# Moving the small loads, copies and GpSimd work of a two-layer attention kernel to the heads of their blocks

## The chip, the cores and the metric

The kernel runs on one core of a Trainium2 chip. The metric is the device time of one execution, in microseconds (us); times of several executions are given by their median. The engines are named as the profile names them: PE (TensorE, matmuls; PEld is its weight load), DVE (VectorE), ACT (ScalarE), POOL (GpSimd), and SP, which here only issues DMAs.

## The reference

The input x is 1 x 32 x 128 x 256 in float32: 4096 tokens of 256 numbers. Layer 0 is an attention over all tokens that is masked by the time index t (0 to 127), with 8 heads of 32; layer 1 is a windowed attention followed by 8 small networks ("experts") with a soft choice between them. Cut to what matters:

```python
# layer 0: h is x, 4096 tokens
q   = layernorm(h) @ wq.T + bq + sym_emb[n]
Q   = q @ wQ.T + bQ ;  K = h @ wK.T + bK ;  V = h @ wV.T + bV      # 8 heads
s   = Q K^T / sqrt(32), -inf where t(key) > t(query)
h   = h + alpha * (softmax(s) V @ out_w.T + out_b)
# layer 1: t is h as 32 sequences of 128 tokens
xl  = layernorm(t)
z   = (relu(xl K xl^T + bias) - 10000 outside a band of 24) * temperature
t   = t + softmax(z) xl
xf  = layernorm(t);  w = softmax(mean over sequences(xf) @ Wr + br)  # 8 experts
for e in range(8):
    a = relu(batchnorm(xf @ W1[e] + b1[e])); a = relu(batchnorm(a @ W2[e] + b2[e]))
    t = t + w[e] * (a @ Wo[e] + bo[e])
```

## The kernel before

**Layer 0.** The tokens are reordered by time, so that the mask is nearly block triangular, and the 4096 queries are taken in 8 blocks b of 512 columns (BLK). The heads are two groups g of four. A unit (b, g) goes over the key tiles of 128 keys that its block may see; one key tile of one group is a step. Both units of block 0 make 6 steps, those of the later blocks 13, 21, 29, 37, 45, 53 and 61.

The order of all engines' work is written out by hand: one loop with the counter n issues, at each round,

- `scores(n)`: 16 matmuls (L1330), those of the first head into the PSUM tile sa (one bank, one buffer), those of the other three into sb (three banks, two buffers);
- `product(n-2)`: 8 or 16 matmuls of the exponentials with the values (L1420), into av;
- `exps(n)`: ACT's two exponentials of sa (L1343) and sb (L1345) into pt, a ring of five SBUF buffers; in a step on the diagonal, POOL then sets the masked parts of pt to zero (L1357);
- `add(n-1)`: DVE adds pt to the unit's running sum acc (L1406), in two halves of the heads, from which the row sums come; the round in which a unit's first two tiles are added also adds what the previous unit carried over (the branch `k == 1` with `more`);
- the next pieces of `todo`, a chain of generators with work for later blocks, then statistics of the layernorm (rounds 0 to 9), and last the jobs that were set for this round: `close_sums` (row sums, one round after a unit's end), `invert` (their reciprocal, six rounds after) and `scale` (twelve rounds after).

Each engine works through its own instructions in this order, and so does each queue of DMAs, SP's and POOL's among them. The pieces of `todo` are spread over a block by this line, where `own` is the number of steps of the block and `at_step` the place in it:

```python
while done < count * at_step // own and not (closing and b):
    next(todo, None)
    done += 1
```

In each block the chain begins with `prep(b + 1)`, four pieces that transpose and project the next block (the PSUM tiles pst, psk, psv, psq). In block 2 `output_weights` follows: a piece that loads wo_n, alpha and outb, one that transposes wo_n into the bank pair ps_wo (L1213) and copies it to woT, and one that copies the values' bias to bvb (L1222) and multiplies it with woT into ps_ob (L1225). In block 3 `expert_norms` follows: a piece that first calls `window()` (the loads of temp and abias; POOL's memset, two selections and three arithmetic operations for bandb, negb and negt, L1238 to L1248; two memsets of the sides of big_t, L1250) and then issues ten loads of bn (L1259), and a piece that transposes bn into psbn (L1263) and copies it to bnT (L1266). A piece takes its banks from the ring of sb (`banks`), so that it stands in the way of the scores until its reader has copied it. The tile wo_n shares a ring of four SBUF buffers (`tok`) with the loads of later blocks' tokens (xg).

The standard deviations of the 24 tiles that come last are taken in `root_rstd`: DVE adds 1e-5 to the variances (L1542), ACT takes the square root and loads its table of exponentials again (L1545). It is called in the first round after the last statistics in which a piece of `todo` is due. `send_rstd` and `invert` then send vectors through DRAM and back by SP (the DMAs rstd, rb, flat, rec and r), to turn columns into rows.

**Layer 1.** It goes over the blocks again, 512 tokens and 8 experts each. `Layer` makes the two hidden layers of an expert (psh, L2076); `combine` multiplies with Wo into psy (L2137), two tiles of 128 tokens in one bank, and DVE adds the weighted result to the tokens (L2145); after the last expert the tokens are stored (L2150). The windowed attention and the layernorms of later blocks are jobs with a cost and a list of needed jobs; `insert` puts them between the matmuls of the experts. It keeps a clock `now` of planned time and takes a job only when each needed job was planned at least `later` (3.2 us, 4.7 at a block's last expert) before:

```python
if all(done_at.get(q, now) + later <= now for q in needs if q in known):
```

So the planner, and not only the text, decides the order of layer 1 on each engine.

## Time and profile before

| | |
|---|---|
| time, median of 3 runs | 1494.84 us (1494.55 to 1494.99) |
| time of the profiled execution | 1492.53 us |
| its span in the profile | 1490.7 us |
| mean granted clock of PE | 0.994 |
| busy in the span: PE | 1457.9 us, 98% |
| DVE | 1201.1 us, 81% |
| ACT | 936.5 us, 63% |
| POOL | 159.5 us, 11% |
| DMA traffic | 110.15 MB |

The span is what the profiler saw between the first and the last instruction; the time of the same execution is 1.83 us longer. Busy shares are means over stages of different kinds: layer 0 takes about the first half of the span, and in it DVE and ACT are nearly as busy as PE. The clock is the share of full speed that the throttle granted to PE. Where it is below 1, PE is busy for longer with the same work.

### The profile page before, as it was taken

To read this page: it belongs to the slowest core of one execution; us is meant where nothing else is said; L and a number is where in the kernel's file an instruction comes from. 1 tells how busy PE (TensorE), PEld (TensorE's weight loads), DVE (VectorE), ACT (ScalarE), POOL (GpSimd) and SP (SyncE) were. 2 spreads that over 40 slices of the span, in tenths; PEclk is the share of its full clock that TensorE was granted. 3 is DMA by queue.
4 is the path that set the end of the run, shared out by engine and by line. 5 is a ranking of instruction groups with operands and counts; after the bars stand their busy time and mean duration, and the time that the engine had idled before them with its cause. 6 is when DMAs were issued, how large, how long until landed. Compare 5 with 4: busy or idle time off the path is not lost.

```text
span 1490.7 us, 23636 instructions
## 1 busy us (share of the span) xinstructions
PE 1457.9 (98%) x8873; PEld 842.3 (56%) x8873; DVE 1201.1 (81%) x2189; ACT 936.5 (63%) x1357; POOL 159.5 (11%) x318
## 2 busy tenths in 40 slices
PE   9999999999999999999899999999999999999998
PEld 5333232232322232222557888888888888888887
DVE  4777788989999999999746787777777777777775
ACT  4776777879889879989454444445445544544443
POOL 2110112100200200000063012020011000000000
PEclk9999999999999999999999999999999999999999
DMA  6220101021000000000332333333433334334442
GB/s 136 51 45 19 30 10 30 9 41 39 1 15 23 1 9 1 8 9 1 119 119 94 121 121 110 120 115 122 134 112 124 106 121 138 112 121 125 130 148 66
DMA packets 96378, 110.15 MB, mean 74 GB/s; under 512 B 17950, under 2 KB 85233, under 8 KB 96257
## 3 DMA queue, kind: packets, MB, share of 16 engines
q1 hardware_dynamic: 93280, 106.87, 24.2%
q8 instruction: 72, 1.18, 0.4%
q0 software_dynamic: 1888, 0.91, 0.2%
q10 hardware_dynamic: 1088, 0.79, 0.2%
q14 instruction: 50, 0.40, 0.1%
HBM read 98.87 MB, written 8.53 MB: 72 GB/s over the span
## 4 chain that ended last, share of the span: by engine, by line
PE 83%; DVE 9%; ACT 4%; issue 2%; DMA 1%; POOL 1%; SPq 0%; ACTq 0%; DVEq 0%; POOLq 0%
PE psh L2076 22%; PE sa L1330 15%; PE av L1420 15%; PE psy L2137 13%; DVE acc L1406 2%; PE psv L1039 2%; PE psq L1012 2%; PE psk L1825 2%; PE psk L993 2%; PE sums L1450 1%; ACT h L2059 1%; PE sb L1330 1%; PE psh L2081 1%; PE pso L1515 1%; PE pss L1837 1%
## 5 line engine op out<-in xcount | busy, mean ns | idle before, releaser
L1406 DVE TENSOR_TENSOR acc<-acc,pt 128x1024 f32<-128x1024 f32 (+2 forms) x470 | 518.1, 1168 | 31.5 <-POOL pt L1357 16.2
L1345 ACT ACTIVATE pt<-sb 128x1536 f32<-128x1536 f32 (+1 forms) x265 | 382.6, 1444 | 1.7 <-PE sb L1330 1.7
L1330 PE MATMUL sa<-q,kT 32*128 32x512 f32 (+3 forms) x576 | 298.8, 605 | 4.5 <-ACT pt L1343 3.6
L1330 PE MATMUL sb<-q,kT 32*128 32x512 f32 (+3 forms) x1728 | 302.0, 604 | 0.0
L2059 ACT ACTIVATE h<-h,bshift,bscale 128x256 f32<-128x256 f32 x244 | 159.2, 699 | 219.1 <-DVE h L2118 219.0
L1420 PE MATMUL av<-pt,v 128*32 128x512 f32 (+3 forms) x2304 | 284.0, 573 | 3.3 <-POOL pt L1357 2.6
L2137 PE MATMUL psy<-wo,h 128*128 128x256 f32 x1024 | 243.6, 381 | 0.0
L2137 PEld LDWEIGHTS psy<-wo,h 128*128 128x128 f32 x1024 | 191.6, 190 | 31.9 <-issue 5.9
L1330 PEld LDWEIGHTS sa<-q,kT 32*128 32x128 f32 x576 | 86.7, 184 | 211.9 <-ACT pt L1343 176.7
L1343 ACT ACTIVATE pt<-sa 128x512 f32<-128x512 f32 (+1 forms) x265 | 158.2, 597 | 73.2 <-PE sb L1330 44.4
L1420 PEld LDWEIGHTS av<-pt,v 128*32 128x32 f32 x2304 | 48.0, 108 | 202.9 <-issue 178.0
L2145 DVE SCALAR_TENSOR_TENSOR tokens<-psy,w,tokens 128x256 f32<-128x256 f32 x256 | 111.0, 475 | 29.1 <-PE psy L2137 28.7
L2103 DVE TENSOR_TENSOR u<-psh,u 128x256 f32<-128x256 f32 x122 | 51.2, 420 | 100.6 <-ACT u L2102 100.3
L1357 POOL MEMSET pt<- 32x256 f32 (+4 forms) x123 | 52.3, 425 | 603.3 <-ACT pt L1345 526.4
L2059 ACT ACTIVATE h<-psh,bshift,bscale 128x256 f32<-128x256 f32 (+1 forms) x132 | 75.8, 576 | 49.7 <-PE psh L2076 43.3
L1330 PEld LDWEIGHTS sb<-q,kT 32*128 32x128 f32 x1728 | 91.0, 184 | 5.1 <-ACT pt L1345 3.8
L2076 PE MATMUL psh<-tx,s 128*128 128x256 f32 x366 | 89.1, 379 | 0.3 <-DVE tx L2049 0.3
L2102 ACT COPY u<-psh 128x256 f32<-128x256 f32 x122 | 43.9, 361 | 72.0 <-PE psh L2076 71.7
L2076 PE MATMUL psh<-th,s 128*128 128x256 f32 x366 | 89.0, 379 | 0.0
L2118 DVE TENSOR_TENSOR h<-psh,u 128x512 f32<-128x512 f32 x122 | 83.1, 681 | 3.2 <-PE psh L2076 3.0
L2076 PEld LDWEIGHTS psh<-tx,s 128*128 128x128 f32 x366 | 69.4, 190 | 10.2 <-DVE tx L2049 0.7
L2076 PEld LDWEIGHTS psh<-th,s 128*128 128x128 f32 x366 | 69.5, 190 | 9.5
(343 smaller groups left out, 1779.1 us busy)
## 6 DMA issues: line engine op xcount, KB each, us to landing
w<-in_L_ffn_W_dram SPq DMA_DIRECT2D x128, 256.0 KB
s<-kept SPq DMA_DIRECT2D x56, 512.0 KB
wo<-in_L_ffn_Wo_dram SPq DMA_DIRECT2D x64, 256.0 KB
xg<-in_x_dram SPq DMA_DIRECT2D x32, 128.0 KB
tokens<-in_x_dram SPq DMA_DIRECT2D x8, 512.0 KB
kept<-s SPq DMA_DIRECT2D x8, 512.0 KB
out_dram<-tokens SPq DMA_DIRECT2D x32, 128.0 KB
rec<-flat SPq DMA_DIRECT2D x60, 64.0 KB
```

What stands on the lines that cost most here:

```text
L1330: nc.tensor.matmul((sb[:, h - 1, :] if h else sa)[:, at : at + w], lhsT=kT[rows, gg, j * P : (j + 1) * P], rhs=q[rows, gg, lo : lo + w], s ...
L1343: nc.scalar.activation(pt[:, 0, used], sa[:, used], AF.Exp, scale=SCALE)
L1345: nc.scalar.activation(pt[:, 1:, used], sb[:, :, used], AF.Exp, scale=SCALE)
L1357: nc.gpsimd.memset(rows, 0.0)
L1406: nc.vector.tensor_tensor(acc[:, hs, cols], acc[:, hs, cols], pt[:, hs, at : at + w], op=ALU.add,)
L1420: nc.tensor.matmul(av[h * HD : (h + 1) * HD, lo : lo + w], lhsT=v[:, j, (g * HG + h) * HD : (g * HG + h + 1) * HD], rhs=pt[:, h, at : at + w],
L2059: nc.scalar.activation(dst, src, AF.Relu, bias=bshift[:, m, k : k + 1], scale=bscale[:, m, k : k + 1])
L2076: nc.tensor.matmul(ps, lhsT=w, rhs=x, start=start, stop=True, skip_group_check=True)
L2103: nc.vector.tensor_tensor(u, a[:, 1], u, op=ALU.add)
L2118: nc.vector.tensor_tensor(flat.rearrange("p (k c) -> p k c", k=2), self.q, self.u.unsqueeze(1).to_broadcast([P, 2, HB]), op=ALU.add,)
L2137: nc.tensor.matmul(ps[:, i, :], lhsT=ht[:, c, r * P : (r + 1) * P], rhs=wo[k][:, c, :], start=(c == 0), stop=(c == 1),)
L2145: nc.vector.scalar_tensor_tensor(out=tokens(n), in0=ps[:, i, :], scalar=w[:, r, e : e + 1], in1=tokens(n), op0=ALU.mult, op1=ALU.add,)
```

## The change

Seven edits; none changes what is computed, and the number of instructions on each engine stays the same.

1. The two memsets of big_t's sides move from `window()` to the head of the program.
2. `output_weights` is started at the head of block 2 (`next(more)`): its loads are issued there, and the bvb copies, now in its first piece, too. The count of block 2's pieces goes from 8 to 7. The pieces stand now after 3, 6, 9, 12 (prep), 15 and 18 of its 21 steps; before, after 3, 6, 8, 11 (prep), 14 (loads), 16 and 19.
3. `expert_norms` is started at the head of block 3, and its first piece now holds the twelve loads alone. POOL's work of `window()` comes after the copy of bnT. The count goes from 7 to 6: after 5, 10, 15, 20 (prep) and 25 (psbn and `window`) of 29 steps; before, after 5, 9, 13, 17 (prep), 21 (loads and `window`) and 25 (psbn).
4. In `add`, the four additions of a unit with carried sums are issued first for both halves of the one column range, then for both of the other.
5. The addition of 1e-5 to the variances is issued right after the last statistics instead of in `root_rstd`.
6. In `combine` of the last expert of the last block each of the two tiles has a bank of its own.
7. In layer 1's planner the jobs that need a "square" wait at least 6.0 us of planned time, those that need a "normalise" at least 4.7 us. This moves some transposes and small products of block 1 by one to three places among PE's instructions; layer 1's other blocks keep their order.

```diff
@@ -886,6 +886,8 @@
 
 
     big_t = big.tile([P, 2, NT + 2 * SIDE], F32, name="big_t")
+    for z in (0, SIDE + NT):
+        nc.gpsimd.memset(big_t[:, :, z : z + SIDE], 0.0)
 
 
     tok = ctx.enter_context(tc.tile_pool(name="tok", bufs=4))
@@ -1206,6 +1208,9 @@
             )
             nc.sync.dma_start(out=alpha, in_=row(ins["L0_conv_alpha"]).to_broadcast([P, 1]))
             nc.sync.dma_start(out=outb, in_=row(ins["L0_conv_out_b"]).to_broadcast([P, D]))
+            bvb = px.tile([P, 2, P], F32, tag="bvb", name="bvb", bufs=1)
+            for c in range(2):
+                nc.vector.tensor_copy(bvb[:, c, :], colT[:, c, 6:7].to_broadcast([P, P]))
             yield
             pss = banks("ps_wo", 2)
             for c in range(2):
@@ -1217,9 +1222,6 @@
                 nc.scalar.copy(woT[:, c, :], pss[c][:, :D])
             nc.vector.tensor_scalar(woT, woT, alpha, None, op0=ALU.mult)
             yield
-            bvb = px.tile([P, 2, P], F32, tag="bvb", name="bvb", bufs=1)
-            for c in range(2):
-                nc.vector.tensor_copy(bvb[:, c, :], colT[:, c, 6:7].to_broadcast([P, P]))
             ps = banks("ps_ob", 1)[0][:, :D]
             for c in range(2):
                 nc.tensor.matmul(
@@ -1232,8 +1234,6 @@
 
         def window():
 
-            nc.sync.dma_start(out=temp, in_=row(ins["L1_attn_temperature"]).to_broadcast([P, 1]))
-            nc.sync.dma_start(out=abias, in_=row(ins["L1_attn_bias"]).to_broadcast([P, 1]))
             nc.gpsimd.memset(bandb, 0.0)
             nc.gpsimd.affine_select(
                 out=bandb, in_=bandb, compare_op=ALU.is_ge, fill=-10000.0,
@@ -1246,12 +1246,11 @@
             nc.gpsimd.tensor_scalar(bandb, bandb, abias, None, op0=ALU.add)
             nc.gpsimd.tensor_scalar(negb, abias, -1.0, None, op0=ALU.mult)
             nc.gpsimd.tensor_scalar(negt, temp, -1.0, None, op0=ALU.mult)
-            for z in (0, SIDE + NT):
-                nc.gpsimd.memset(big_t[:, :, z : z + SIDE], 0.0)
 
         def expert_norms(banks):
 
-            window()
+            nc.sync.dma_start(out=temp, in_=row(ins["L1_attn_temperature"]).to_broadcast([P, 1]))
+            nc.sync.dma_start(out=abias, in_=row(ins["L1_attn_bias"]).to_broadcast([P, 1]))
             t = px.tile([NB, D], F32, tag="bn", name="bn", bufs=1)
             for l in range(2):
                 for k, s in enumerate(bn_names):
@@ -1264,6 +1263,7 @@
                     ps[:, c * NB : (c + 1) * NB], t[:, c * P : (c + 1) * P], ident[:NB, :NB]
                 )
             nc.vector.tensor_copy(bnT.rearrange("p c k -> p (c k)"), ps[:, : 2 * NB])
+            window()
             yield
 
 
@@ -1384,6 +1384,7 @@
                                 live[b, g][:, hs, :z], first[:, hs, :z], pt[:, hs, :z],
                                 op=ALU.add,
                             )
+                        for hs in HEADS:
                             nc.vector.tensor_tensor(
                                 live[b, g][:, hs, z:], live[b, g][:, hs, z:], pt[:, hs, z:],
                                 op=ALU.add,
@@ -1539,9 +1540,6 @@
 
             def root_rstd():
                 cols = slice(2 * TPB, NTILE)
-                nc.vector.tensor_scalar(
-                    rstd0[:, cols], mean0[:, cols, 1], 1e-5, None, op0=ALU.add
-                )
                 nc.scalar.activation(rstd0[:, cols], rstd0[:, cols], AF.Sqrt)
                 ready(AF.Exp)
 
@@ -1591,9 +1589,13 @@
                         if b == 0:
                             todo, count = itertools.chain(rest_of_first(), todo), 8
                         if b == 2:
-                            todo, count = itertools.chain(todo, output_weights(banks)), 8
+                            more = output_weights(banks)
+                            next(more)
+                            todo, count = itertools.chain(todo, more), 7
                         if b == 3:
-                            todo, count = itertools.chain(todo, expert_norms(banks)), 7
+                            more = expert_norms(banks)
+                            next(more)
+                            todo, count = itertools.chain(todo, more), 6
                         if 2 <= b < NBLK - 2:
                             xblk[b + 2] = load_x(b + 2, "xg")
                     scores(b, g, k)
@@ -1645,6 +1647,10 @@
                     for sb_, si in stat_at.get(n, ()):
                         stats(sb_, si, xstat[sb_])
                         if (sb_, si) == (NBLK - 1, TPB - 1):
+                            cols = slice(2 * TPB, NTILE)
+                            nc.vector.tensor_scalar(
+                                rstd0[:, cols], mean0[:, cols, 1], 1e-5, None, op0=ALU.add
+                            )
                             due = 1
                     if 1 < b < NBLK - 1 and not g and k == 1:
                         send_rstd(b + 1)
@@ -2130,12 +2136,17 @@
         b, e = work[k]
         w = blk[b]["w"]
         dst = out[0].rearrange("n t d -> (n t) d")
-        ps = bank(f"psy{k}_{r2}").rearrange("p (k d) -> p k d", k=2)
+        if k < len(work) - 1:
+            ps = bank(f"psy{k}_{r2}").rearrange("p (k d) -> p k d", k=2)
+            pss = [ps[:, i, :] for i in range(2)]
+        else:
+
+            pss = [bank(f"psy{k}_{r2}_{i}")[:, :D] for i in range(2)]
         for i in range(2):
             r = 2 * r2 + i
             for c in range(2):
                 nc.tensor.matmul(
-                    ps[:, i, :], lhsT=ht[:, c, r * P : (r + 1) * P],
+                    pss[i], lhsT=ht[:, c, r * P : (r + 1) * P],
                     rhs=wo[k][:, c, :],
                     start=(c == 0), stop=(c == 1),
                 )
@@ -2143,7 +2154,7 @@
             r = 2 * r2 + i
             n = b * TPB + r
             nc.vector.scalar_tensor_tensor(
-                out=tokens(n), in0=ps[:, i, :], scalar=w[:, r, e : e + 1],
+                out=tokens(n), in0=pss[i], scalar=w[:, r, e : e + 1],
                 in1=tokens(n), op0=ALU.mult, op1=ALU.add,
             )
             if e == E - 1:
@@ -2379,7 +2390,7 @@
 
 
 
-    jobs, done_at = [], {}
+    jobs, done_at, slow = [], {}, {}
 
     def job(name, cost, f, *needs):
         jobs.append((name, cost, f, needs))
@@ -2471,6 +2482,10 @@
             job("bound_flags", 0, bound_flags, "bound_sums")
             job("bound_verdict", 0, bound_verdict, "bound_flags")
     jobs = [j for j in jobs if j[0] not in done_at]
+    for name in bound_of:
+        slow["square", name] = 6.0
+    for n in range(NTILE):
+        slow["normalise", n] = 4.7
 
 
 
@@ -2512,7 +2527,7 @@
             if cost and spent >= allowed():
                 k += 1
                 continue
-            if all(done_at.get(q, now) + later <= now for q in needs if q in known):
+            if all(done_at.get(q, now) + max(later, slow.get(q, 0)) <= now for q in needs if q in known):
                 f()
                 now += cost
                 spent += cost
```

## The prediction

> **What bounds the kernel now.** I read the page's shares first, then its chain, then TensorE's waits, and then short windows of time around those waits.

> ```profile
> PE 1457.9 (98%) x8873; PEld 842.3 (56%) x8873; DVE 1201.1 (81%) x2189; ACT 936.5 (63%) x1357; POOL 159.5 (11%) x318
> ...
> PE 83%; DVE 9%; ACT 4%; issue 2%; DMA 1%; POOL 1%; SPq 0%; ACTq 0%; DVEq 0%; POOLq 0%
> ```

> TensorE (PE) is busy for 98% of the span and carries 83% of the chain. The change removes no matmul, so it can save only PE's idle time, 32.8 us in all, and time in which PE's clock was cut. The waits of PE up to 700 us show which idle time the edits touch (total, times, longest, in us):

> ```profile
> PE sa L1330 <- ACT pt L1343: 3.6, 4, 2.0
> PE ps_ob L1225 <- DVE bvb L1222: 3.0, 1, 3.0
> PE av L1420 <- POOL pt L1357: 2.6, 1, 2.6
> PE ps_wo L1213 <- DMA wo_n<-in_L_conv_out_w_dram: 2.0, 1, 2.0
> ```

> The diff moves the releaser of each of these: 2.04 + 3.01 + 2.61 + 1.97 = 9.63 us of idle. The windows add what follows a stall (columns: PE, PEld, DVE, ACT, POOL busy, granted clock, DMA share, GB/s):

> ```profile
> 72.00:74.00 2.00, 1.39 (x12) 0.47 (x16) 0.00 (x0) 2.00 (x4) 0.04 (x1) 1.00 0.13 1
> ...
> 146.00:148.00 2.00, 2.00 (x22) 1.19 (x24) 1.09 (x2) 0.65 (x3) 0.00 (x0) 0.62 0.02 6
> 148.00:150.00 2.00, 2.00 (x12) 0.34 (x14) 1.67 (x2) 1.93 (x2) 0.00 (x0) 0.53 0.00 0
> ...
> 158.00:160.00 2.00, 2.00 (x8) 0.84 (x9) 0.91 (x3) 0.00 (x0) 0.00 (x0) 0.50 0.00 0
> ...
> 232.00:234.00 2.00, 1.75 (x16) 0.58 (x16) 1.77 (x2) 0.00 (x0) 0.20 (x1) 0.50 0.52 136
> 234.00:236.00 2.00, 2.00 (x14) 0.81 (x10) 1.86 (x3) 0.00 (x0) 0.00 (x0) 0.50 0.89 245
> 236.00:238.00 2.00, 2.00 (x12) 0.20 (x8) 2.00 (x4) 1.32 (x2) 0.00 (x0) 0.50 0.15 7
> ```

> After three of the four stalls PE counts as fully busy but works at half speed for 3.4 to 6.8 us: the stall is paid a second time. After the gap of 2.04 us (ending at 72.61) the clock stayed at 1.00.

> [...]

> ```profile
> 217.91 11.44 DVE L1406 TENSOR_TENSOR acc<-acc,pt 128x1024 f32<-128x1024 f32 x10
> 222.66 7.25 POOL L1246 TENSOR_SCALAR bandb<-bandb,abias 128x160 f32<-128x160 f32 x1 [12.82 <-DMA abias<-in_L_attn_bias_dram]
> ```

> The adds end at 229.35, the POOL operation at 229.91; DVE's reciprocal of 229.27 stands between. Behind it in POOL's queue were two small operations, two memsets of big_t and the diagonal step's three memsets of pt (1.63 us from 230.56), for which both av and the next add waited. [...]adds on the same half follow each other at 0.60 us, as independent ones do.

> **The change part by part.** Gains are minus times of one execution.

> *Variances' constant (root_rstd).* Now DVE's addition of 1e-5 is issued just before the square root, behind other DVE work:

> ```profile
> 68.97 0.17 DVE L1542 TENSOR_SCALAR rstd<-mean 128x24 f32<-128x24 f32 x1
> 69.18 0.22 ACT L1545 ACTIVATE rstd<-rstd 128x24 f32<-128x24 f32 x1 [2.06 <-DVE rstd L1542]
> ```

> ScalarE (ACT) stood for 2.06 us, so its exponential of sa, which frees the only sa bank, was late and PE stood for 2.04 at 72.61. With the addition right after the last statistics ACT runs on; the exponentials behind move up by 2.06 and PE is left with at most 0.2 of idle. ACT's table load (1.28) stays. **1.9** (0.5, if ACT's backlog takes it, to 2.0).

> *Layer 0's output weights.* The loads of wo_n, alpha and outb (issue 0.58 + 0.47 + 0.43 us) move from block 2's step 14 to its head, some 30 us earlier; wo_n took 3.1 us from issue to landing, so the wait of 1.97 goes. The bvb copies (2 x 0.18) stand now behind five adds that end at 156.7, and go to the head as well: the 3.01 go. Each stall's slow stretch goes too: 146 to 150 at 0.62 and 0.53 cost 2 x 0.38 + 2 x 0.47 = 1.7; 156.6 to 160.1 at about 0.5 cost 1.6. Sum 8.3. New waits: ps_wo and ps_ob now come at steps 15 and 18 rather than 16 and 19; each takes a slot of the scores' three-bank ring until ACT has copied (2 x 0.33) or DVE's outb operation, queued behind add(17), has read. Going through the steps at 2.07 us with these waits, step 21's scores start at 154.1 rather than 161.58, with 0.4 us of idle before step 20. **7.5** (4, if DVE's lag keeps half of the second stall, to 8). On SP wo_n's group passes ahead of block 4's x load, rstd(3) and reciprocals, 1.5 us in all; these have over 10 us until use. wo_n takes a ring slot whose earlier tile is read by then. Step 14 loses its piece, and the keys', values' and queries' pieces come one step later: 0.

> *Layer 1's constants.* Loads of temp, abias and ten of bn (12 issues, 219.29 to 223.81: 4.5 us) go to block 3's head; psbn comes at step 25 as before, but the POOL chain is issued after psbn's copy, so the diagonal step's memsets (step 23) stand ahead of it. Removed: 2.61 of idle and the half clock of 232 to 238.7, 6.7 x 0.5 = 3.4; 6.0 together. Added: psbn's bank is held by a copy queued behind DVE's add(24), and DVE lags here, since the queries' four DVE operations (2.75) come at step 20, three steps before the diagonal. I work out 0.8 for step 26 (ACT) and 1.3 for step 27 (bnT's copy). And POOL's bandb operation may interleave with DVE's adds instead of waiting: elsewhere adds beside such operations took 1.22 instead of 0.69; three to four would cost up to 1.7, of which I take half. 6.0 − 0.8 − 1.3 − 0.9 = **3.0** (−1.5 to 4.0). The chain must be done by step 29's memsets, about 11 us after it may start; a gap such as the reciprocal's lets it in. If it doesn't, the same wait returns there.

> *Planner.* The dictionary slow makes the jobs that need a square wait 6.0 us and those that need a normalisation 4.7, rather than 3.2. In the order of instructions this moves transposes and small products of block 1 by one to three places. PE's waits after 768 us:

> ```profile
> PE ptx L1813 <- ACT big_t L1817: 0.8, 1, 0.8
> PE psf L2171 <- DVE tokens L2018: 0.6, 1, 0.6
> PE ptx L1813 <- ACT xl L1797: 0.5, 1, 0.5
> ```

> The waits of ptx are of this kind: 1.3 to win, with a chance that a job pushed later meets another. **0.8** (−0.5 to 1.3).

> *Last combine.* The two tiles of the last half share a bank, and DVE's pair began 0.04 us after PE's last matmul:

> ```profile
> 1483.92 0.88 DVE L2145 SCALAR_TENSOR_TENSOR tokens<-psy,w,tokens 128x256 f32<-128x256 f32 x2 [0.85 <-PE psy L2137]
> ```

> With own banks the first (0.44) runs beside the second tile's matmuls. [...] **0.45** (0 to 0.9).

> *big_t's sides* (0.18 us on POOL) go to the program's head, ahead of POOL's first loads: 0 to −0.2; I take 0, PE waits there for weights that SP loads. *Order of the carried adds*: 0, by the spacing above.

> **Sum.** 1.9 + 7.5 + 3.0 + 0.8 + 0.45 = 13.65 against this execution's 1492.53 (span 1490.7 and 1.83 around it), that is 1478.9. It lies 2.3 below the median of its runs, 1494.84; from the median the forecast is 1494.84 − 13.65 = **1481.2**.

> **The rivals.**
> 1. *The stall of layer 1's constants only moves.* POOL's chain again meets DVE's adds, or bnT's copy waits longer: a gap of 2 us and the half clock again. That part is then −1.3, not 3.0: gain 9.35, **1485.5**. For it: DVE is at 24 to 25 us of each 25 from 325 us on, and the chain's ten-instruction wait above. Against it: its deadline is 11 us off.
> 2. *DVE is the bound inside a block.* A step costs PE 2.07 us and DVE two adds of 1.17; PE's stalls let DVE catch up. Then half of the output weights' gain (3.75) and all of the constants' gain are lost: 13.65 − 6.75 = 6.9, **1487.9**. Against it: five pt buffers are about 10 us of slack at PE's pace, and diagonal steps and unit ends give DVE time.
> 3. *Slower: SP's queue.* Twelve loads (4.5 us) stand at block 3's head ahead of block 5's x, rstd(4) (whose write and read back took 8.1 us: 164.83 to 172.89), rb(4) and the row sums r(2,1), 2.9 us. DVE runs in order, so its reciprocal of r(2,1) stops every add. I place that reading 0 to 1 us after it is due. It decides only if it is later than DVE's slack of about 4 us plus the gains, some 17 us; at 20 us late the time is 1494.84 − 13.65 + 16 = 1497.2 and, with one half-clock window of 3.4 us behind the gap (1.7 more), **1498.9**.
> 4. *It doesn't act*: loads issued at the head are held by SP's in-order waits until they land no earlier, and the copies stay behind the same adds. **1494.8.** Against it: SP is idle for long stretches at both heads.

> **How the numbers follow.** My forecast 0.55, rival 1 0.23, rival 2 0.12, rival 3 0.05, rival 4 0.03; 0.02 for other harm. The forecast's own range is 1478.5 to 1484.5 from the parts' bounds, not all bad at once. For 8 in 10 the range must take in rival 1 and the middle of rival 2: 1478.0 to 1489.0. About 0.2% (3.0 us) is what a measurement here can tell from no change: faster than 1491.85 is 0.55 + 0.23 + 0.12 = 0.90, within 0.04 (rival 4 and a little), slower 0.06.

> **What would show it.** Right: no PE wait on wo_n, bvb or POOL's pt; clock 1.00 from 140 to 245 us in the windows; ACT's square root without a wait on DVE; the last DVE operation about 0.45 us after PE's end. Wrong: a PE wait of 2 us or more on sb or av near step 27 or 29 of block 3 with a clock of 0.5 behind it; adds of 1.2 us beside POOL's bandb; a DVE wait on r from SP's queue early in block 3; new ptx or psf waits after 775 us.

## The result, and the profile after

The changed kernel takes 1478.39 us (median of 4 runs, 1477.89 to 1480.14) against 1494.91 (4 runs, 1494.55 to 1495.11): ratio 0.9892, 95% interval 0.9875 to 0.9909. The gain is 16.5 us; 13.65 were forecast. The profiled execution took 1477.89 us with a span of 1476.1, 14.6 less than the span before. That the medians differ by more than the spans comes from the two profiled executions: that of before lay 2.3 below its median, that of after 0.5.

The page's shares and three of PE's waits up to 700 us (total, times, longest), after; the others, 1.4 us at the longest, stand in the profile before as well:

```profile
PE 1454.4 (99%) x8873; PEld 842.4 (57%) x8873; DVE 1198.8 (81%) x2189; ACT 936.6 (63%) x1357; POOL 153.1 (10%) x318
```

```profile
PE sa L1330 <- ACT pt L1343: 0.7, 2, 0.4
PE sums L1451 <- DVE acc L1407: 0.6, 1, 0.6
PE sb L1330 <- DVE bnT L1265: 0.5, 1, 0.5
```

The four waits of 2 to 3 us are gone. One new wait has come, on bnT, and it is of the kind that was priced. The windows at the places of the old stalls (PE, PEld, DVE, ACT, POOL busy, clock, DMA share, GB/s) show the full clock:

```profile
146.00:148.00 2.00, 2.00 (x12) 0.91 (x12) 1.30 (x2) 0.94 (x1) 0.67 (x1) 1.00 0.00 0
148.00:150.00 2.00, 2.00 (x25) 1.01 (x24) 1.97 (x4) 1.87 (x2) 0.00 (x0) 1.00 0.00 0
...
222.00:224.00 2.00, 2.00 (x14) 0.68 (x16) 1.86 (x3) 1.40 (x2) 1.83 (x4) 1.00 0.14 34
224.00:226.00 2.00, 2.00 (x10) 0.37 (x10) 2.00 (x2) 1.45 (x1) 0.04 (x1) 1.00 0.60 163
```

The last two show how a busy PE can hide a wait: between 222 and 226 it counts as busy throughout, with 14 and 10 matmuls where the windows of 2 us from 150 to 300 us that count as busy throughout hold 19 on the mean. What counts is the distance between rounds (a round is one step's turn of the loop). Taking ACT's exponential of sb (L1345) of each round as the mark, and subtracting the two traces, the distance between the kernels grows like this:

| place | before less after, us | forecast |
|---|---|---|
| head of the program (DMA landing times) | 0.25 | 0 |
| block 1: square root | 2.06 | 1.9 |
| block 2: output weights | 7.56 | 7.5 |
| block 3: layer 1's constants | 2.13 | 3.0 |
| block 6, start of its second unit: carried adds | 0.9 | 0 |
| layer 1, block 1: planner | 1.0 | 0.8 |
| tail | 0.75 | 0.45 |
| sum | 14.65 | 13.65 |

The square root is now free of DVE, whose addition stands 3 us ahead of it in the timeline after:

```profile
63.92 0.18 DVE L1651 TENSOR_SCALAR rstd<-mean 128x24 f32<-128x24 f32 x1
...
66.88 0.22 ACT L1543 ACTIVATE rstd<-rstd 128x24 f32<-128x24 f32 x1
```

POOL's addition on bandb, 7.25 us before, now takes 1.26, and bnT's copy comes 4.4 us after the transposes (221.78) whose result it copies:

```profile
222.26 1.26 POOL L1246 TENSOR_SCALAR bandb<-bandb,abias 128x160 f32<-128x160 f32 x1
226.16 0.32 DVE L1265 COPY bnT<-psbn 128x160 f32<-128x160 f32 x1
226.53 1.13 PE L1330 MATMUL sb<-q,kT 32*128 32x512 f32 x6 [0.49 <-DVE bnT L1265]
```

PE's two longest waits in layer 1 after 768 us: the two of ptx are gone, and one of psa is new.

```profile
PE psa L1896 <- ACT ptl L1887: 1.4, 1, 1.4
PE psh L2082 <- DVE h L2111: 1.0, 3, 0.4
```

### The profile page after: what moved, and what is told of

Read it like the earlier page. It is cut to its first block, busy times and chain, and to the rows that moved or that the text cites. A ratio compares the mean times of both kernels' runs of the same rounds, so it can differ in the third digit from the quotient of the medians.

```text
span 1476.1 us, 23637 instructions
## 1 busy us (share of the span) xinstructions
PE 1454.4 (99%) x8873; PEld 842.4 (57%) x8873; DVE 1198.8 (81%) x2189; ACT 936.6 (63%) x1357; POOL 153.1 (10%) x318
## 3 DMA queue, kind: packets, MB, share of 16 engines
q8 instruction: 72, 1.18, 0.3%
## 4 chain that ended last, share of the span: by engine, by line
PE 82%; DVE 10%; issue 3%; ACT 3%; DMA 1%; SPq 0%; DVEq 0%; POOL 0%; ACTq 0%; POOLq 0%
PE psh L2082 22%; PE sa L1330 14%; PE av L1421 14%; PE psy L2148 13%; DVE acc L1407 3%; PE psv L1041 2%; PE psk L995 2%; PE psq L1014 2%; PE psk L1831 2%; PE sums L1451 1%; PE sb L1330 1%; ACT h L2065 1%; PE psh L2087 1%; PE pso L1516 1%; PE pss L1843 1%
## 5 line engine op out<-in xcount | busy, mean ns | idle before, releaser
L1345 ACT ACTIVATE pt<-sb 128x1536 f32<-128x1536 f32 (+1 forms) x265 | 382.8, 1445 | 3.0 <-PE sb L1330 2.9
L1330 PE MATMUL sb<-q,kT 32*128 32x512 f32 (+3 forms) x1728 | 299.8, 600 | 0.5 <-DVE bnT L1265 0.5
L1330 PE MATMUL sa<-q,kT 32*128 32x512 f32 (+3 forms) x576 | 296.5, 600 | 1.9 <-ACT pt L1343 0.7
L1330 PEld LDWEIGHTS sa<-q,kT 32*128 32x128 f32 x576 | 85.8, 183 | 205.8 <-ACT pt L1343 171.6
L1343 ACT ACTIVATE pt<-sa 128x512 f32<-128x512 f32 (+1 forms) x265 | 157.8, 595 | 63.1 <-PE sb L1330 29.1
L1357 POOL MEMSET pt<- 32x256 f32 (+4 forms) x123 | 52.2, 424 | 609.1 <-ACT pt L1345 508.1
L1330 PEld LDWEIGHTS sb<-q,kT 32*128 32x128 f32 x1728 | 90.1, 183 | 7.3 <-ACT pt L1345 4.3
```

The costliest lines, as they stand in the source:

```text
L1330: nc.tensor.matmul((sb[:, h - 1, :] if h else sa)[:, at : at + w], lhsT=kT[rows, gg, j * P : (j + 1) * P], rhs=q[rows, gg, lo : lo + w], s ...
L1343: nc.scalar.activation(pt[:, 0, used], sa[:, used], AF.Exp, scale=SCALE)
L1345: nc.scalar.activation(pt[:, 1:, used], sb[:, :, used], AF.Exp, scale=SCALE)
L1357: nc.gpsimd.memset(rows, 0.0)
```

## The experiments

All start from the changed kernel. Distances are by the same marks against its trace, with the head's offset (up to 1 us, from when the first loads land) taken off; times are of single executions unless a median is named.

**u_const: block 3's constants as before.**

```diff
             nc.sync.dma_start(out=abias, in_=row(ins["L1_attn_bias"]).to_broadcast([P, 1]))
+            window()
...
             nc.vector.tensor_copy(bnT.rearrange("p c k -> p (c k)"), ps[:, : 2 * NB])
-            window()
...
-                            more = expert_norms(banks)
-                            next(more)
-                            todo, count = itertools.chain(todo, more), 6
+                            todo, count = itertools.chain(todo, expert_norms(banks)), 7
```

> The changed kernel with edit 3 alone undone (loads and GpSimd's chain at step 21 of block 3, before psbn; count 7), but without the two memsets of big_t in the chain. My reading of the two traces: block 3's constants gained 2.1 us, as 3.2 at the stall less 1.1 because the queries' piece came three steps later. Then the span is 2.0 to 2.5 longer than the changed kernel's 1476.1, PE waits again for about 2.3 us on pt from POOL with a clock of 0.5 behind it, the loss of this block lies within it, and everything after block 3 keeps its distance. Rival: the stall came back only together with the late stalls of block 2 (DVE's backlog); then there is no PE wait on POOL and the span changes by under 0.5.

Measured: 1481.06 us, span 1479.3. Block 3 loses 1.0 us, not 2.0 to 2.5; 1.6 more of the span is lost in layer 1 at 760 us, where the clock fell to 0.50 in this execution (from 761.0 to 764.4). PE waits for POOL, after POOL was held by DVE's adds as before:

```profile
PE av L1421 <- POOL pt L1357: 2.5, 1, 2.5
```

```profile
212.97 7.26 POOL L1246 TENSOR_SCALAR bandb<-bandb,abias 128x160 f32<-128x160 f32 x1 [12.80 <-DMA abias<-in_L_attn_bias_dram]
...
219.60 0.24 DVE L1490 RECIPROCAL r<-r 128x16 f32<-128x16 f32 x1
```

```profile
220.00:222.00 2.00, 0.00 (x0) 0.00 (x0) 0.00 (x0) 1.93 (x2) 1.80 (x6) 1.00 0.05 4
222.00:224.00 2.00, 1.55 (x22) 0.88 (x26) 1.57 (x2) 0.00 (x0) 0.39 (x1) 1.00 0.49 129
224.00:226.00 2.00, 2.00 (x17) 0.40 (x14) 1.86 (x3) 1.10 (x2) 0.00 (x0) 1.00 0.78 217
```

The wait is there without block 2's stalls, so the rival falls. But with a gap of 2.5 us the clock stays at 1.00 here, where it halved for 6.8 us after 2.6 in the kernel before; the last section shows what differs. That half clock was worth only about 1.1 us (2.13 against 1.0): with PE at full speed it waits for psbn's bank instead.

**psq17: the queries' piece at step 17 again.**

```diff
             yield
+            yield
             ps = banks("psbn", 1)[0]
...
-                            todo, count = itertools.chain(todo, more), 6
+                            todo, count = itertools.chain(todo, more), 7
```

> The changed kernel with count 7 for block 3 and an empty piece ahead of psbn: the queries' piece is at step 17 again as before, psbn and the POOL chain stay at step 25. If the later place of the queries' piece cost 1.1 us, block 3 ends 0.9 to 1.2 us earlier and bnT's copy waits less for DVE (PE's wait on bnT under 0.5). Rival: the loss belongs to psbn and its bank alone; then block 3 ends within 0.2 of the changed kernel.

Measured: 1476.54 us. Block 3 shortens by 1.6 us, more than expected, and there is no PE wait on bnT. With the count of 7 the keys' and the values' pieces move too (to steps 9 and 13), but the distance is back at 0.0 after each of them; the 1.1 below comes with the queries' piece. The rounds of block 3 say where. Time from one exponential of sb to the next, summed, in us:

| kernel | 13 rounds, to steps 13 to 25 | three rounds, to steps 26, 27 and 28 | all |
|---|---|---|---|
| before | 35.0 | 7.02 + 3.01 + 2.10 | 47.2 |
| u_const | 35.0 | 4.91 + 3.53 + 2.57 | 46.0 |
| after | 36.1 | 2.69 + 3.67 + 2.57 | 45.0 |
| psq17 | 35.0 | 2.69 + 3.15 + 2.57 | 43.4 |
| bn_act | 36.1 | 2.69 + 2.52 + 2.12 | 43.4 |
| best | 35.0 | 2.69 + 2.52 + 2.11 | 42.4 |

Three free rounds take 6.2. The kernel after loses 1.1 in the earlier rounds, where its queries' matmuls (3.7 us of PE) stand at step 20 instead of 17, and 0.5 at bnT, because DVE has the queries' four operations to do three steps before.

**bn_act: bnT copied by ACT.**

```diff
-            nc.vector.tensor_copy(bnT.rearrange("p c k -> p (c k)"), ps[:, : 2 * NB])
+            nc.scalar.copy(bnT.rearrange("p c k -> p (c k)"), ps[:, : 2 * NB])
```

> The changed kernel with bnT copied by ACT instead of DVE. If psbn's bank is late because its copy stands behind DVE's adds, the rounds of steps 26 to 28 shorten: 1.3 us less (0.8 to 1.8) at block 3's end and no PE wait on bnT; what stays is the wait of step 26 for the bank (0.8). Rival: ACT is the tighter engine there and its exponentials are pushed back by the copy of 0.3; then the gain is under 0.4.

Measured: 1477.49 us; block 3 shortens by 1.6, all of it in the last two of the three rounds. The bank was late because its copy stood behind DVE's adds; ACT copies it at once and its exponentials aren't pushed back in this block; 0.2 of the gain is lost again in block 4's first rounds, so that layer 0 is 1.4 shorter.

**u_wts and u_copy: block 2's output weights.** In u_wts all of edit 2 is undone, in u_copy only the bvb copies go back:

```diff
-            bvb = px.tile([P, 2, P], F32, tag="bvb", name="bvb", bufs=1)
-            for c in range(2):
-                nc.vector.tensor_copy(bvb[:, c, :], colT[:, c, 6:7].to_broadcast([P, P]))
             yield
             pss = banks("ps_wo", 2)
...
             yield
+            bvb = px.tile([P, 2, P], F32, tag="bvb", name="bvb", bufs=1)
+            for c in range(2):
+                nc.vector.tensor_copy(bvb[:, c, :], colT[:, c, 6:7].to_broadcast([P, P]))
             ps = banks("ps_ob", 1)[0][:, :D]
```

> The changed kernel with edit 2 alone undone (loads at step 14 of block 2, copies at step 19; count 8). The traces put 7.45 us on it. Expected: span longer by 7.2 to 7.7, PE waits of 2.0 on wo_n and 3.0 on bvb, a clock of 0.5 to 0.7 for about 3.4 us behind each. Rival: [...]with the stalls coming 2 us earlier one of the two half-clock stretches is missing, and the loss is 5.5 to 6.

> The changed kernel with only the bvb copies moved back to the piece of ps_ob (step 18 now); the loads stay at the head. If the two stalls of block 2 are separate, this costs the second alone: a PE wait on bvb of up to 3.0 and 1.6 of half clock, 3.5 to 4.6 us in the span. Rival: the copies wait only because DVE lags behind PE's first stall and its slow stretch; then the PE wait on bvb is under 1.5 us without a fall of the clock, and the loss is under 1.5.

Measured: u_wts 1489.66 us, block 2 longer by 8.9; u_copy 1485.39, longer by 5.5. PE's waits in block 2 of u_wts, then of u_copy, and the windows behind the latter's:

```profile
PE ps_ob L1227 <- DVE bvb L1224: 3.1, 1, 3.1
PE ps_wo L1215 <- DMA wo_n<-in_L_conv_out_w_dram: 1.8, 1, 1.8
```

```profile
PE ps_ob L1227 <- DVE bvb L1224: 3.6, 1, 3.6
```

```profile
148.00:150.00 2.00, 0.43 (x1) 0.46 (x2) 1.52 (x4) 0.00 (x0) 0.00 (x0) 0.55 0.00 0
150.00:152.00 2.00, 2.00 (x8) 1.17 (x11) 0.35 (x1) 0.00 (x0) 0.00 (x0) 0.50 0.04 8
152.00:154.00 2.00, 2.00 (x12) 0.26 (x12) 2.00 (x3) 0.35 (x1) 0.00 (x0) 0.50 0.00 0
```

The two stalls are separate: the copies alone bring theirs, in full and with half clock. Both runs lose more than expected (7.7 and 4.6 were the upper ends), since the half clock lasted 6.8 us behind the second stall rather than 3.4, and in u_copy the wait itself was 0.6 longer. The rivals, that the loss would be smaller, fall.

**u_root: the addition of 1e-5 in root_rstd again.**

```diff
             def root_rstd():
                 cols = slice(2 * TPB, NTILE)
+                nc.vector.tensor_scalar(
+                    rstd0[:, cols], mean0[:, cols, 1], 1e-5, None, op0=ALU.add
+                )
                 nc.scalar.activation(rstd0[:, cols], rstd0[:, cols], AF.Sqrt)
...
-                            cols = slice(2 * TPB, NTILE)
-                            nc.vector.tensor_scalar(
-                                rstd0[:, cols], mean0[:, cols, 1], 1e-5, None, op0=ALU.add
-                            )
```

> The changed kernel with edit 5 alone undone. The traces put 2.05 us on it: ACT's square root waits 2.06 for DVE, PE 2.04 for sa. Expected: span longer by 2.0 to 2.1 with the clock at 1.00, or by 3.5 to 3.8 if [...]this gap halves the clock. Rival: none of it was this edit, and the difference of 2.05 at this place came from the head of the program; then 0.

Measured: 1483.76 us. Layer 0 loses 2.05 at the gap and 1.6 behind it, the second of the two outcomes: the same gap as in the kernel before, with the clock halved.

```profile
72.00:74.00 2.00, 1.30 (x12) 0.41 (x16) 0.00 (x0) 2.00 (x4) 0.00 (x0) 0.90 0.13 1
74.00:76.00 2.00, 2.00 (x9) 0.34 (x10) 0.00 (x0) 1.91 (x2) 1.79 (x4) 0.50 0.00 0
76.00:78.00 2.00, 2.00 (x8) 1.69 (x9) 1.64 (x5) 0.00 (x0) 0.25 (x1) 0.75 0.10 8
```

The rest of its span is lost in layer 1 at 842 us, by the clock again (0.50 from 841.59 to 845.00).

**u_add and add_rev: the order of the carried adds.** In u_add the loops are one again (A0 B0 A1 B1):

```diff
-                        for hs in HEADS:
                             nc.vector.tensor_tensor(
                                 live[b, g][:, hs, z:], live[b, g][:, hs, z:], pt[:, hs, z:],
```

In add_rev the two loops change places (B0 B1 A0 A1).

> The changed kernel with edit 4 alone undone (order A0 B0 A1 B1). Between the traces the distance grows by 0.9 us at the start of block 6, where GpSimd's operations of with_bias alternate with DVE's adds. My theory: the adds take as long in either order, but A0 and A1 are the last readers of the unit's first pt tile; as first and second instead of first and third they free it one add (1.14) earlier, and ACT's next exponential waited for that buffer. Then this run loses 0.9 (0.7 to 1.0) at block 6's first unit and nothing elsewhere in layer 0. Rival: the order is worth nothing (what I predicted), and the 0.9 came from how DVE and GpSimd happened to meet; then no loss there.

> The changed kernel with the two loops of edit 4 in reverse: B0 B1 A0 A1. The first pt tile is then freed by the fourth add. If the early release is the cause, the loss at block 6 is that of A0 B0 A1 B1 and one more add of 1.14: about 2.0 us (1.7 to 2.2). If the order of the adds doesn't matter, 0.

Measured: u_add 1480.64 us, 0.9 lost at the start of block 6's second unit (at 508 us; the expectations call it the first) and nothing elsewhere in layer 0; add_rev 1481.03, 1.6 lost there. Most of the rest of both spans is lost in layer 1, where the clock fell to 0.50 (u_add from 838.6, add_rev from 761.4 us on). What ACT waits for at that place, in the kernel after, u_add and add_rev:

```profile
ACT pt L1343 <- PE sb L1330: 0.6, 2, 0.5
```

```profile
ACT pt L1343 <- DVE acc L1383: 1.6, 1, 1.6
```

```profile
ACT pt L1343 <- DVE acc L1388: 2.2, 1, 2.2
```

The later the last reader of the first pt tile, the longer ACT waits for the buffer. The rival falls. The size in add_rev is 1.6 instead of 2.0, since the fourth add no longer met POOL's operations, which end at 508.07 there: it took 0.7 us and not 1.2, and ACT's exponential starts 0.7 later than in u_add instead of 1.14. The order doesn't cost wherever POOL slows the adds: at the start of block 5's second unit (386 to 391 us) the four took 1.1 to 1.2 us as well, and neither run lost anything there, since ACT wasn't waiting for the buffer.

**u_l1: planner and last combine as before.**

```diff
-        slow["square", name] = 6.0
-        slow["normalise", n] = 4.7
...
-        if k < len(work) - 1:
+        if True:
```

> The changed kernel with edits 6 and 7 undone (planner and the last combine), whose places are apart in time. The traces put 1.0 us on the planner, in block 1 of layer 1, and 0.75 on the tail. Expected in the profile: the two waits of ptx (0.8 and 0.5) are back, the wait of psa (1.4) near 836 us is gone, DVE's last pair runs after PE's end for 0.88; span longer by 1.0 + 0.75. Rival: the planner only trades one wait for the other: with psa's wait gone the loss of the planner's part is under 0.3, and since that gap of 1.4 us sometimes halves the clock for 1.6 us more, the timed runs differ from the changed kernel's 1478.4 by less than the traces say.

Measured: median 1479.93 us (4 runs, 1479.80 to 1481.33), ratio to before 0.9916 (0.9899 to 0.9932). This interval overlaps that of the changed kernel, so that the times alone don't tell the two apart. In the profile ptx's two waits are back and psa's is gone; the planner's part is 0.76 us, the tail's 0.4 by DVE's end:

```profile
1471.49 0.88 DVE L2156 SCALAR_TENSOR_TENSOR tokens<-psy,w,tokens 128x256 f32<-128x256 f32 x2 [0.85 <-PE psy L2148]
```

In the kernel after the last are single ones:

```profile
1469.19 0.48 DVE L2156 SCALAR_TENSOR_TENSOR tokens<-psy,w,tokens 128x256 f32<-128x256 f32 x1 [0.38 <-PE psy L2148]
1470.05 0.48 DVE L2156 SCALAR_TENSOR_TENSOR tokens<-psy,w,tokens 128x256 f32<-128x256 f32 x1 [0.38 <-PE psy L2148]
```

By the profiles the planner is worth something net of the wait it brings, 0.8 to 1.0; the rival's 0.3 is too low. (From the last exponential of layer 0 to PE's end the four executions with this planner, the psa wait and the full clock agree within 0.03 us, so that 0.8 is clear of their spread.) The other 0.35 of the tail in the table above comes in the last stores and needs no cause in the edits: from DVE's end to the span's end the fourteen executions took 5.5 to 6.0 us, the kernel before 5.95 and the kernel after 5.56.

**win_head: POOL's work right at block 3's head.**

```diff
             nc.sync.dma_start(out=abias, in_=row(ins["L1_attn_bias"]).to_broadcast([P, 1]))
+            window()
             t = px.tile([NB, D], F32, tag="bn", name="bn", bufs=1)
...
-            window()
```

> The changed kernel with window() called at the head of block 3, right behind its loads, instead of after bnT's copy. GpSimd's addition on bandb then meets DVE's stream of adds as soon as abias has landed. Theory: it is held off as long as DVE issues two-input adds back to back, and let in at the first gap; at the block's head there are gaps (diagonal step, unit end), so it lasts under 4 us, nothing waits for it and the time stays within 0.3 of the changed kernel. Rival: it is held for as long as in the kernel before (over 7 us) and the first diagonal step's memsets and av wait behind it, 2 us or more.

Measured: 1478.18 us; block 3 is 0.2 shorter than in the kernel after. POOL is held only until the add that runs has ended (159.57), since DVE then stands for 1.39 us:

```profile
159.00 1.12 POOL L1246 TENSOR_SCALAR bandb<-bandb,abias 128x160 f32<-128x160 f32 x1 [0.51 <-DMA abias<-in_L_attn_bias_dram]
```

So it matters little whether POOL's chain stands behind bnT's copy; it must only not stand where DVE has a backlog of adds and a diagonal step is near, as in the kernel before and in u_const, where its addition took 7.25 and 7.26 us and not 1.12. What POOL meets beside unbroken adds this run doesn't test.

**best and best_p4.** best is psq17 and bn_act together; best_p4 adds one line to the planner:

```diff
         slow["normalise", n] = 4.7
+    slow["weights", 4] = 4.7
```

> The queries' piece back at step 17 and bnT copied by ACT together. Alone they gained 1.6 and 1.4 us in block 3, but the wait on bnT was gone with the first alone, so they overlap: 1.8 us less than the changed kernel (1.5 to 2.4), 1476.6 in the median. If they added up it would be 3.0.

> As the last, and the planner waits 4.7 instead of 3.2 us for the weights of pair 4, so that psa's matmuls come later than the copies they wait for. If the gap of 1.4 us is only an early place, it goes and with it the half clock that follows it in some runs: 1.2 to 1.6 less in a profile, 1.5 to 2.5 in the median. Rival: the bound there is ACT, and the wait comes back at the next matmul: under 0.3.

Measured: best 1476.08 us (4 runs, 1475.82 to 1477.54), ratio to before, whose 7 runs beside it had a median of 1492.88, 0.9886 (0.9870 to 0.9903). Block 3 is 2.7 us shorter than in the kernel after, more than the expected 2.4 at most: 1.1 of psq17 and the 1.6 of bn_act, only bnT's 0.5 is common to both. best_p4: 1475.66 us (1475.03 to 1477.78), 0.9887 (0.9871 to 0.9904). Its wait on psa is gone, but another has come:

```profile
PE psy L2149 <- DVE fro L2208: 1.0, 1, 1.0
```

Layer 1 gains 0.24, as the rival said, though by DVE and not ACT. The timed runs tell neither from the other, and neither from the kernel after: the ratios to before overlap (that of after is 0.9875 to 0.9909), and the lower times belong to a series in which the kernel before, too, was 2.0 us faster. That best gains 2.7 in block 3 is shown by the profile alone.

## Why the prediction was right, and where it was off

The mechanism and most sizes were right: 1478.39 lies in the range of 1478.0 to 1489.0, near its lower end, and 0.1 below the narrower range that was given for the forecast itself.

- **The four stalls with their slow stretches.** Right. No PE wait on wo_n, bvb or POOL's pt is left, and the clock is 1.00 through both stretches. Going through block 2's steps gave 7.5; the traces show 7.56. That they meet so closely is luck in part: with edit 2 undone (u_wts) the loss was 8.9, since the half clock behind the second stall lasted 3.4 us longer.
- **The square root.** 1.9 forecast, 2.06 shown. That this gap costs no clock was a reading of one execution; in u_root it cost 1.6 more.
- **Layer 1's constants.** 3.0 forecast, 2.13 shown. At the stall itself the forecast (6.0 less 3.0) meets the rounds (12.13 less 8.93, that is 3.20), but not term by term. The new waits for ACT and bnT came to 2.7 (8.93 less 6.2), where 0.8 and 1.3 were taken; the interleaving of POOL with DVE, taken as 0.9, cost about 0.2 (win_head, which has POOL's work elsewhere, is shorter by that). The term that was missing is the queries' piece at step 20: its effect on DVE's lag was seen, the 1.1 us that it costs PE's rounds was not priced at all. The working also misread one line: the ten adds stand from 217.91 on, and POOL's addition, which starts at 222.66 in the fifth, waited for six of them and not for ten.
- **Order of the carried adds.** Priced at 0 because adds follow each other at 0.60 us in either order. That is right for DVE and the wrong question: the order decides when the first pt tile is free for ACT. It was worth 0.9 at one of the two units where POOL's operations slow these adds.
- **Planner.** 0.8 forecast, 0.8 to 1.0 shown; the chance that a later job meets another came true with psa's 1.4.
- **Tail.** 0.45 forecast, 0.4 shown for DVE; the 0.35 in the stores is within the play of that stretch (5.5 to 6.0 us).
- **The base.** The terms' sum was 1.0 short; the other 1.8 of the error are the forecast's base, since the terms were taken from an execution 2.3 below its median and set against that median, and the profiled execution of after lay only 0.5 below its own. How much of the 16.5 belongs to the change is open by as much: in other series the kernel before took 1495.47, 1493.05 (single executions) and 1492.88 us (median of 7), and win_head, which is the kernel after but for POOL's place, was 14.7 faster than the last of these.
- **Rivals.** The stall didn't move (rival 1): what is left at bnT is 0.5 of recorded wait and brings no half clock. DVE was not the bound (rival 2): of the output weights' gain nothing was lost. The reciprocals were not late by the loads on SP (rival 3): the rounds at block 3's start are those of before. The loads and copies did act (rival 4): the waits on wo_n and bvb are gone.

## What to carry to other kernels

Price a stall as its idle time plus what the clock takes behind it, but know that the second part comes in one execution and not in the next: behind a gap of 2.04 us it was 1.6 us in u_root and nothing in the kernel before. A gain read from one profile has that much play. Here it came or not by where the gap lay among the switching times of the clock (below). When small side work is moved, look at every engine that it passes, and give it to the engine that has no backlog there: who frees a shared bank or ring buffer, and behind what that engine's instruction stands, decided the sizes here, also where the order of equal work looked free. A share of busy time doesn't show such waits; the distance from round to round does.

## What the runs showed of the hardware

```profile
70.18:73.59 3.41, 1.36 (x16) 0.31 (x8) 1.53 (x3) 3.40 (x6) 0.00 (x0) 1.00 0.24 43
73.59:77.00 3.41, 3.41 (x15) 1.26 (x12) 0.64 (x2) 2.32 (x3) 2.04 (x5) 0.50 0.06 5
```

```profile
67.97:71.38 3.41, 2.60 (x26) 0.88 (x24) 3.41 (x5) 2.17 (x4) 0.00 (x0) 1.00 0.35 77
71.38:74.79 3.41, 2.18 (x17) 0.58 (x18) 0.24 (x2) 3.41 (x6) 0.80 (x2) 1.00 0.07 1
74.79:78.20 3.41, 3.41 (x16) 2.84 (x16) 1.92 (x5) 0.94 (x1) 1.25 (x4) 1.00 0.06 5
```

```profile
218.25:221.66 3.41, 1.72 (x16) 0.31 (x8) 1.59 (x3) 3.29 (x4) 3.21 (x5) 1.00 0.03 2
221.66:225.08 3.42, 2.63 (x30) 1.09 (x34) 2.52 (x3) 0.45 (x2) 0.73 (x1) 1.00 0.51 141
```

- Between the first switch and the end of layer 0 every such stretch with 1.83 us or more of PE's idle time was followed by the half clock (seven, in before, u_root, u_wts and u_copy; those of before had 1.96, 2.72 and 2.16 us), and behind none with 1.69 or less did the clock fall. The half clock then lasted one stretch or two, 3.4 or 6.8 us; why two is open.
- In layer 1, at about 760 or 840 us, seven of the thirteen profiled executions of the changed kernel and its variants show a half clock, and lose 1.6 to 1.9 us by it. The recorded idle time alone doesn't sort these stretches, but the place does. At about 760 us each of the thirteen has a gap of 0.59 and, 1.6 us behind it, one of 0.31. In the five where both lie in one stretch (u_const, u_wts, u_copy, add_rev, best) the clock was halved; in the other eight it was not, and in after, for one, a stretch ends at 758.04 us between the two. The 1.4 us before psa was followed by the half clock in two of eleven, u_root and u_add, where the gap begins 0.3 and 0.1 us behind a stretch's start; in psq17, where it begins 0.4 behind, it was not. What else in the stretch counts with the gap is open.
- POOL's addition on bandb ended 0.55 to 0.56 us after the DVE add behind which DVE's row of adds (acc<-acc,pt) first broke: at 229.91 behind 229.35 (before), 220.23 behind 219.67 (u_const), 223.52 behind 222.97 (after, where the break is only 0.03 us) and 160.13 behind 159.57 (win_head). So it took 7.25 and 7.26 us where six adds came first, and 1.26 and 1.12 where one did. POOL isn't held for each of its instructions, though. Of six additions of outb in the kernel after, the first took 3.25 us (383.01 to 386.26; DVE's row broke at 385.66), and the others (0.73 to 1.18 us each) then ran in turn with DVE's adds:

```profile
383.01 8.49 POOL L906 TENSOR_TENSOR tokens<-tokens,outb 128x256 f32<-128x256 f32 x6
386.39 2.25 DVE L1383 TENSOR_TENSOR acc<-pt,pt 128x512 f32<-128x512 f32 x2 [0.73 <-ACT pt L1345]
388.56 2.35 DVE L1388 TENSOR_TENSOR acc<-acc,pt 128x512 f32<-128x512 f32 x2
```
